# Dense passes and the first routing between the first attention and the routed tiles

## The chip, the cores and the metric

The kernel runs on one core of a Trainium2 chip. The metric is the device time of one execution in microseconds (us). The engines are named as in the profile: PE (matrix multiplies; PEld is its weight load), DVE (vector), ACT (activations), POOL (general purpose), SP (issues most DMAs).

## The reference

Two layers of gated cross attention, each followed by a mixture of experts, on 16 sequences of 112 tokens of width 256 (1792 tokens), with a context of 375 rows for each sequence:

```python
x = x + tanh(g_xattn[0]) * L0_xattn(layernorm(x), ctx)   # 16 heads of 16
x = x + tanh(g_ffn[0])   * L0_ffn(layernorm(x))
x = x + tanh(g_xattn[1]) * L1_xattn(layernorm(x), ctx)   # one head of 256
x = x + tanh(g_ffn[1])   * L1_ffn(layernorm(x))
```

The change lies in and around `L0_ffn`. It has 14 routed experts, of which each token takes two, and 2 shared ones that every token passes through. Each expert is RMS norm, 256 to 512, SiLU, 512 to 256:

```python
gates = softmax(xf @ router_w)                 # 14 logits for each token
top_v, top_i = top_k(gates, 2)                 # scattered into masked, then normalised
routed_out = einsum('end,ne->nd', routed, masked)
shared = sum over the 2 shared experts of silu(h @ W1) @ W2
```

## The kernel before

All arithmetic is float32. Tokens lie in `x_sb` in 14 tiles of 128. For the shared experts the tiles are grouped in `blocks`: (0, 4), (4, 4), (8, 4), (12, 2), that is first tile and number of tiles. One *pass* is one shared expert over one block. It consists of pieces:

- `hidden_piece` (L472): 128 of the 512 hidden columns for a block. PE multiplies into a bank (L476), ACT applies Silu into `hT` (L480). Four of them (`KH`) make a pass's hidden half.
- `output_piece` (L482): one token tile of the block. PE multiplies `hT` by the second weights (L486), DVE adds the result to `x_sb` (L490). There are as many as the block has tiles.

A float32 matmul appears as two records in the profile. A hidden piece is 4 records of L476, an output piece 8 of L486. `hT` comes from a pool with two buffers.

**First attention.** It runs as 64 steps (`last` = 64), one for each sequence and group of four heads, and some more steps that empty the pipeline. In a step `n` the order of every engine's queue is written out: scores of step `n`, work registered for place 0, `apply` of step `n - 2`, place 1, place 2, `maxima`, `turned_scores(n - 1)` (PE, then four Exp on ACT, L649), place 3. Extra work is registered with `at(step, place, ...)`. Near the end these are: `project(12)` at step 65 and `project(13)` at step 67, place 2 (L692; PE L695, DVE L699); `first_turn` of the last sequence at step 66 and `second_turn` at step 67 (L670, L682); `measured1` (statistics on DVE and powers on POOL), `normed1` (DVE, and an SP store to `xn_rows`), `turned1` (two PE transposes, an ACT copy to `xT`) and `logits` (PE, ACT into `lg0`) for each token tile; those of the last tile come at steps 67, 69, 70 and 71.

PSUM banks in a step come from `bank()` (L528). At place 2 the first three requests of a step get banks 0, 1 and 3 of the two pairs that hold the scores in full steps; a pair is one tile of two banks.

One pass, shared expert 0 over block 0, is placed in steps 65 to 72, a piece for each step (L748 to L752).

**Between attention and the routed tiles** (L907 to L952). Here nothing is pinned: a planner orders the instructions by their place in the program and by what is ready, and may also move them in between the written ones ahead. The pieces of three passes are mixed with the routing:

- `two_largest` (L239): for each token the two largest logits as one-hot rows, on DVE.
- `places` (L290): counts by matmuls (L302, L305), from them on DVE the owner of each of `TILES0` = 41 tiles of 128 rows (`owner_i`) and the row of each token (`at_i`).
- `takers` (L348): one-hot matrices on DVE (L395, L380, L386) and 56 records of small matmuls (L404) give the token in each row (`taker`).
- `gates_of` (L263): the two gate values, with one Exp on ACT (L277).

The three passes are expert 0 over block 1, expert 1 over block 0, expert 1 over block 1, with `places` behind the first pass's hidden pieces and `takers` behind the second's.

**Routed tiles** (`routed`, L851). For each tile SP loads the owner's weights (L858; it needs `owner_i`), POOL gathers 128 rows of `xn_rows` (L860; it needs `taker`), PE transposes them (L867), DVE scales (L869), then hidden (L879, L884), output (L891, L893) and a store. Tile t + 1 is fetched and transposed ahead of tile t's hidden matmuls. The weights pool has six buffers, of which the two shared experts keep two. The first 36 tiles always run, the last 5 only if needed.

After that the second layer's products, the four remaining passes over blocks 2 and 3 (`rest`), the second attention and its experts follow.

Of the kernel before, what the change touches and what calls it, by code (L numbers as in the profile page):

```python
# [19 lines left out]
NT = N // P  # L20
# [5 lines left out]
ER, ES = 14, 2  # L26
HID = 512
KH = HID // P
E1 = 4

TILES0 = 2 * NT + ER - 1
# [26 lines left out]
def tile_flamingo(  # L58
# [124 lines left out]
    tg = const.tile([P, 4], F32, tag="tg", name="tg")  # L183
# [48 lines left out]
    def at_once(parts):  # L232
        while True:
            try:
                next(parts)
            except StopIteration as end:
                return end.value

    def two_largest(wk, lg, e, nt):  # L239

        sh = [P, nt, e]

        def full(name, shape=sh):
            return wk.tile(shape, F32, tag=f"{name}{e}_{nt}", name=name, bufs=1)

        ohs, tmp, left = full("ohs", [P, nt, 2, e]), full("tmp"), full("left")
        rev = revi[:, ER - e : ER].unsqueeze(1).to_broadcast(sh)
        tops = []
        for r in range(2):
            top, first = full(f"top{r}", [P, nt]), full(f"first{r}", [P, nt])  # L250
            tops.append(top)
            nc.vector.tensor_reduce(top, lg, AX.X, ALU.max)
            nc.vector.tensor_tensor(tmp, lg, bc(top, sh), ALU.is_equal)
            nc.vector.tensor_tensor(tmp, tmp, rev, ALU.mult)
            nc.vector.tensor_reduce(first, tmp, AX.X, ALU.max)
            nc.vector.tensor_tensor(ohs[:, :, r, :], tmp, bc(first, sh), ALU.is_equal)
            if r == 0:
                nc.vector.scalar_tensor_tensor(left, ohs[:, :, 0, :], -3e38, lg, ALU.mult, ALU.add)
                lg = left
                yield  # L260
        return ohs, tops
# [28 lines left out]
    def places(wk, pool, tag, ohs, e, n, nt=NT):  # L290


        def full(name, shape, dtype=F32):
            return wk.tile(shape, dtype, tag=f"{name}{e}", name=name, bufs=1)


        both = full("both", [P, nt + 1, e])
        nc.gpsimd.memset(both[:, nt, :], 0.0)
        nc.vector.tensor_add(both[:, :nt, :], ohs[:, :, 0, :], ohs[:, :, 1, :])
        yield  # L300
        before = pool.tile([P, nt + 1, e], F32, tag=tag, name="before")
        nc.tensor.matmul(before, below, both, start=True, stop=False)  # L302
        for i in range(nt):
            sh = [P, nt - i, e]
            nc.tensor.matmul(  # L305
                before[:, i + 1 :, :], ones, both[:, i : i + 1, :].to_broadcast(sh),
                start=False, stop=(i == nt - 1),
            )
        yield

        own_i = full("own_i", [P, e], I32)
        nc.vector.tensor_scalar(own_i, before[:, nt, :], float(P - 1), None, ALU.add)
        nc.vector.tensor_scalar(own_i, own_i, 7, None, ALU.arith_shift_right)
        own = full("own", [P, e])
        nc.vector.tensor_copy(own, own_i)
        sh = [P, 2, e, e]
        up = full("up", sh)
        nc.vector.tensor_tensor(
            up, own.unsqueeze(1).unsqueeze(1).to_broadcast(sh), below_e[:, :, :e, :e], ALU.mult
        )  # L320
        ends = full("ends", [P, 2, e])
        nc.vector.tensor_reduce(ends, up, AX.X, ALU.add)

        past = full("past", [P, n, e])
        nc.vector.tensor_tensor(
            past, ends[:, 1:2, :].to_broadcast([P, n, e]), bc(marks[:, :n], [P, n, e]), ALU.is_le
        )
        owner = full("owner", [P, n])
        nc.vector.tensor_reduce(owner, past, AX.X, ALU.add)
        owner_i = keep.tile([P, n], I32, tag=f"owner_i{e}", name="owner_i")  # L330
        nc.vector.tensor_scalar(owner_i, owner, float(e - 1), None, ALU.min)
        total_i = keep.tile([P, 1], I32, tag=f"total_i{e}", name="total_i")
        nc.vector.tensor_copy(total_i, ends[:, 1, e - 1 : e])
        yield owner_i, total_i

        spot = full("spot", [P, nt, e])
        nc.vector.tensor_tensor(
            spot, before[:, :nt, :], ends[:, 0:1, :].to_broadcast([P, nt, e]), ALU.add
        )
        sh = [P, nt, 2, e]  # L340
        nc.vector.tensor_tensor(ohs, ohs, spot.unsqueeze(2).to_broadcast(sh), ALU.mult)
        at = full("at", [P, nt, 2])
        nc.vector.tensor_reduce(at, ohs, AX.X, ALU.add)
        at_i = keep.tile([P, nt, 2], I32, tag=f"at_i{e}", name="at_i")
        nc.vector.tensor_copy(at_i, at)
        return at_i
# [96 lines left out]
    blocks = [(t, min(4, NT - t)) for t in range(0, NT, 4)]  # L443
# [25 lines left out]
    def hidden_rows():  # L469
        return dense.tile([P, KH, 4 * P], F32, tag="hT", name="hT")  # L470

    def hidden_piece(new_bank, hT, e, t0, n, m):  # L472
        a = both[e][0]
        ph = new_bank()[:, : n * P]
        for k in range(KD):
            nc.tensor.matmul(  # L476
                ph, a[:, k, m * P : (m + 1) * P], xT[:, k, t0 * P : (t0 + n) * P],
                start=(k == 0), stop=(k == KD - 1),
            )
        nc.scalar.activation(hT[:, m, : n * P], ph, AF.Silu)  # L480

    def output_piece(new_bank, hT, e, t0, j):  # L482
        c, i = both[e][1], t0 + j
        py = new_bank()[:, :D]
        for m in range(KH):
            nc.tensor.matmul(  # L486
                py, hT[:, m, j * P : (j + 1) * P], c[:, m, :],
                start=(m == 0), stop=(m == KH - 1),
            )
        nc.vector.scalar_tensor_tensor(  # L490
            x_sb[:, i, :], py, tg[:, 2:3], x_sb[:, i, :], ALU.mult, ALU.add
        )

# [5 lines left out]
    with tc.tile_pool(name="a0", bufs=2) as a0, tc.tile_pool(  # L502
        name="a0_s", bufs=1, space=PSUM
# [240 lines left out]
        def at(step, where, f, *args):  # L744
            side.setdefault((step, where), []).append((f, args))


        hT = hidden_rows()  # L748
        pieces = [(hidden_piece, (bank, hT, 0, *blocks[0], m)) for m in range(KH)]
        pieces += [(output_piece, (bank, hT, 0, blocks[0][0], j)) for j in range(blocks[0][1])]  # L750
        for n, (f, args) in enumerate(pieces):
            at(last + 1 + n, 2, f, *args)  # L752

        def blank():

# [151 lines left out]
    with tc.tile_pool(name="f0", bufs=3) as f0, tc.tile_pool(  # L907
        name="f0_h", bufs=3, space=PSUM
    ) as ps_h, tc.tile_pool(name="f0_y", bufs=3, space=PSUM) as ps_y, tc.tile_pool(
        name="f0_x", bufs=2, space=PSUM  # L910
    ) as ps_x:
        ohs, tops = at_once(two_largest(f0, lg0, ER, NT))

        def h_bank():
            return ps_h.tile([P, 512], F32, tag="h", name="ph")

        def y_bank():
            return ps_y.tile([P, D], F32, tag="y", name="py")

        def run(units, after=lambda n: None):  # L920
            prev = None
            for n, (e, t0, w) in enumerate([*units, (None, None, None)]):
                if e is not None:
                    hT = hidden_rows()
                    for m in range(KH):
                        hidden_piece(h_bank, hT, e, t0, w, m)
                if prev is not None:
                    for j in range(prev[3]):
                        output_piece(y_bank, *prev[:3], j)
                if e is not None:  # L930
                    after(n)
                prev = (hT, e, t0, w)

        units = [(e, t0, w) for t0, w in blocks for e in range(ES)]
        first, rest = [units[2], units[1], units[3]], units[4:]
        found = {}

        def route(n):
            if n == 0:
                parts = places(f0, ps_x, "x", ohs, ER, TILES0)  # L940
                next(parts)
                next(parts)
                found["owner"], found["total"] = next(parts)
                found["at"] = at_once(parts)
            if n == 1:
                found["taker"] = at_once(
                    takers(f0, ps_x, "x", found["at"], ER, TILES0)
                )

        run(first, route)  # L950
        at_i, owner_i, taker, total_i = (found[name] for name in ("at", "owner", "taker", "total"))
        gates = at_once(gates_of(f0, lg0, tops, ER, NT, 1e-9, tg[:, 2:3]))  # L952

        routed(0, OFTEN0, wpool, f0, ps_h, ps_y, ps_x)

# [742 lines left out]
```

## Time and profile before

| | us |
|---|---|
| runs | 915.47, 921.25, 924.17; median 921.25 |
| profiled execution | 921.77, its span 919.8, mean granted PE clock 0.986 |
| PE busy in the span | 859.0 (93%) |
| DVE, ACT, POOL busy | 468.9, 347.0, 231.5 |
| first dense matmul after the attention's steps (L476, into `ph`) | 357.86 |
| first weight load of a routed tile issued (L858) | 373.66 |
| `taker` written (L417) | 392.72 |
| first transpose of a routed tile (L867, PE) | 414.32 |
| first hidden matmul of a routed tile (L879) | 415.32 |
| last hidden matmuls of the routed tiles | 558.9 |

Times inside the execution count from the start of the span. A row of a timeline has the start, the time from the first record's start to the last one's end, the engine, the line, the operation with output and inputs, the shape and the number of records; in brackets the idle time before it and what ended it. Busy PE is not PE at its peak, since matmuls overlap; the granted clock has to be read beside it.

ACT's rows where it changes between Exp and Silu, in the last attention steps and after them:

```profile
327.73 1.48 ACT L649 ACTIVATE pT<-pt 125x336 f32<-125x336 f32 x4 [0.87 <-PE pt L642]
330.66 0.27 ACT L738 ACTIVATE lg<-pt,rt 128x14 f32<-128x14 f32 x1 [1.46 <-PE pt L734]
330.95 1.28 ACT L480 ACT_TABLE_LOAD   x1
332.42 0.60 ACT L480 ACTIVATE hT<-sp 128x512 f32<-128x512 f32 x1 [0.18 <-PE sp L476]
...
356.39 1.28 ACT L277 ACT_TABLE_LOAD   x1 [3.74 <-DVE g L272]
357.69 0.38 ACT L277 ACTIVATE g<-g 128x210 f32<-128x210 f32 x1
359.92 1.28 ACT L480 ACT_TABLE_LOAD   x1 [1.85 <-PE ph L476]
```

Every change of function set has a load of 1.28 us in ACT's queue.

### The profile page before, as it was taken

The numbers are of one execution on the slowest core, as the hardware profiler recorded it, in microseconds if no ns is written. First come the engines' busy times: TensorE is split into PE (matmuls) and PEld (weight loads), VectorE is DVE, ScalarE is ACT, GpSimd is POOL, SyncE is SP. The second block draws the span as 40 slices with busy tenths as digits, with TensorE's granted clock in tenths as the row PEclk, the third lists the DMA queues.
The fourth block names the chain that finished last, engine by engine and source line by source line (L and its number), as shares of the span: only waits on it lengthen the run. The fifth ranks groups of instructions, "written<-read, shape, count | busy, mean of one in ns | idle before, by whom it ended". The sixth has DMA issues, their size and how long they took to land. (4 is left out here: it accounts for less than half of the span.)

```text
span 919.8 us, 18113 instructions
## 1 busy us (share of the span) xinstructions
PE 859.0 (93%) x7038; PEld 619.4 (67%) x7038; DVE 468.9 (51%) x1240; ACT 347.0 (38%) x851; POOL 231.5 (25%) x435
## 2 busy tenths in 40 slices
PE   6899999999999978999999999989999998999984
PEld 3566666666666645779888887666778776767753
DVE  3666666565566623512222223585556463666557
ACT  2455555555555432111111110223223354445453
POOL 3231221120111111013222213670433313221063
PEclk9999999999999999889999999999999999999998
DMA  7230010001010000406999995322346334899834
GB/s 262 64 94 1 25 47 25 24 24 42 25 41 9 7 9 10 183 24 225 319 318 305 320 302 159 117 69 70 121 121 188 145 138 142 287 318 334 291 82 107
DMA packets 41911, 124.02 MB, mean 135 GB/s; under 512 B 5712, under 2 KB 22224, under 8 KB 33248
## 3 DMA queue, kind: packets, MB, share of 16 engines
q1 hardware_dynamic: 35664, 108.30, 34.9%
q0 software_dynamic: 5616, 14.03, 5.6%
q8 instruction: 56, 0.92, 0.4%
q10 hardware_dynamic: 544, 0.52, 0.2%
q14 instruction: 31, 0.25, 0.1%
HBM read 109.46 MB, written 13.37 MB: 134 GB/s over the span
## 5 line engine op out<-in xcount | busy, mean ns | idle before, releaser
L621 DVE TENSOR_REDUCE mz<-sp 112x2 f32<-112x750 f32 x128 | 114.2, 935 | 56.0 <-PE sp L614 56.0
L649 ACT ACTIVATE pT<-pt 125x336 f32<-125x336 f32 x256 | 94.6, 456 | 65.0 <-PE pt L642 65.0
L207 POOL TENSOR_SCALAR rstd<-mv 128x1 f32<-128x1 f32 (+1 forms) x49 | 12.2, 250 | 300.9 <-DVE mv L200 295.2
L879 PE MATMUL phr<-xgT,wr_sb 128*128 128x128 f32 x576 | 73.2, 280 | 7.5 <-DVE xgT L869 7.5
L879 PEld LDWEIGHTS phr<-xgT,wr_sb 128*128 128x128 f32 x576 | 68.0, 191 | 12.4 <-DVE xgT L869 12.1
L1396 PE MATMUL py<-wr_sb,hT 128*128 128x256 f32 x312 | 76.1, 388 | 0.0
L860 POOL DMA_INDIRECT xg_sb<-xn_rows,taker x36 | 34.3, 954 | 155.6 <-PE px L867 108.4
L884 ACT ACTIVATE hTr<-phr 128x512 f32<-128x512 f32 x36 | 21.5, 597 | 137.1 <-PE phr L879 137.1
L869 DVE TENSOR_SCALAR xgT<-px,wr_sb 128x128 f32<-128x128 f32 x72 | 21.9, 346 | 96.5 <-DMA wr_sb<-in_wr_dram 67.3
L891 PE MATMUL pyr<-wr_sb,hTr 128*128 128x256 f32 x288 | 68.0, 379 | 0.0
L661 PEld LDWEIGHTS pt<-pT,va 125*32 125x32 f32 x1536 | 38.0, 109 | 39.1 <-ACT pT L649 33.6
L1396 PEld LDWEIGHTS py<-wr_sb,hT 128*128 128x128 f32 x312 | 57.8, 195 | 6.6
L642 PE MATMUL pt<-qm,kt 32*125 32x112 f32 x1536 | 61.2, 283 | 0.7 <-ACT kt L546 0.4
L661 PE MATMUL pt<-pT,va 125*32 125x112 f32 x1536 | 58.7, 264 | 2.0 <-ACT pT L649 2.0
L642 PEld LDWEIGHTS pt<-qm,kt 32*125 32x125 f32 x1536 | 49.1, 183 | 15.7 <-issue 11.6
L1385 ACT ACTIVATE hT<-ptz,wr_sb 128x128 f32<-128x128 f32 x156 | 57.9, 449 | 1.6 <-PE ph L1352 1.6
L614 PE MATMUL sp<-kt,qt 32*112 32x375 f32 x512 | 56.6, 494 | 1.2 <-ACT qt L573 0.8
L541 PE MATMUL pt<-ctx_sb,wk 128*128 128x375 f32 x128 | 51.6, 527 | 5.8 <-DMA ctx_sb<-in_ctxT_dram 5.8
L891 PEld LDWEIGHTS pyr<-wr_sb,hTr 128*128 128x128 f32 x288 | 52.0, 190 | 5.6
L199 DVE BATCH_NORM_STATS2 bnst<-ph 128x6 f32<-128x512 f32 x39 | 27.2, 698 | 40.0 <-PE ph L1352 39.1
L546 ACT ACTIVATE kt<-pt,bks,spots 128x375 f32<-128x375 f32 x64 | 39.0, 659 | 22.7 <-PE pt L541 22.7
L476 PE MATMUL ph<-xT,w_sb 128*128 128x512 f32 (+1 forms) x112 | 46.8, 567 | 0.6 <-DVE x_sb L490 0.6
(275 smaller groups left out, 1514.1 us busy)
## 6 DMA issues: line engine op xcount, KB each, us to landing
wr_sb<-in_wr_dram SPq DMA_DIRECT2D x36, 1025.0 KB
wr_sb<-in_wr_dram SPq DMA_DIRECT2D x31, 1028.0 KB
ctx_sb<-in_ctxT_dram SPq DMA_DIRECT2D x32, 375.0 KB
yg<-yr SPq DMA_DIRECT2D x59, 128.0 KB
ctxn_sb<-in_ctxN_dram SPq DMA_DIRECT2D x16, 375.0 KB
xn_rows<-xn SPq DMA_DIRECT2D x24, 128.0 KB
out_dram<-yb SPq DMA_DIRECT2D x10, 128.0 KB
w_sb<-in_w1s_dram SPq DMA_DIRECT2D x2, 512.0 KB
```

The source lines that it names most:

```text
L476: nc.tensor.matmul(ph, a[:, k, m * P : (m + 1) * P], xT[:, k, t0 * P : (t0 + n) * P], start=(k == 0), stop=(k == KD - 1),)
L541: nc.tensor.matmul(pk, wk0_sb[:, k, c * P : (c + 1) * P], ctxs[b][:, k, :], start=(k == 0), stop=(k == KD - 1),)
L546: nc.scalar.activation(kts[b][:, c, u, :], pk, AF.Identity, bias=bks[:, c, u : u + 1], scale=spots[:, 2 + u : 3 + u],)
L614: nc.tensor.matmul(sps[j // 2][:TQ, j % 2, :S], qt[r : r + HP, c, t0 : t0 + TQ], kt[r : r + HP, g, u, :], start=True, stop=True,)
L621: nc.vector.tensor_reduce(mz[:, 2 * h : 2 * h + 2, HD * (1 - u)], sp[:TQ, :, :S], AX.X, ALU.max, negate=True,)
L642: nc.tensor.matmul(sts[j][:SC, s * TQ : (s + 1) * TQ], kt[r : r + HP, c // 2, c % 2, s * SC : (s + 1) * SC], qm[r : r + HP, :], start=True ...
L649: nc.scalar.activation(pT[:, j, :], sts[j][:SC, : NSC * TQ], AF.Exp)
L661: nc.tensor.matmul(po[r : r + HP, :], va[:, s, (c // 2) * 8 + j * 2 + c % 2, :], pT[:, j, s * TQ : (s + 1) * TQ], start=(s == 0), stop=(s ...
L879: nc.tensor.matmul(ph[:, m, :], a[:, k, m * P : (m + 1) * P], xgT[:, k, :], start=(k == 0), stop=(k == KD - 1),)
L891: nc.tensor.matmul(py, hT[:, m, :], c[:, m, :], start=(m == 0), stop=(m == KH - 1))
L1385: nc.scalar.activation(hT[:, m, :], pt[:, m, :], AF.Relu, bias=w[:, c + KH + m : c + KH + m + 1], scale=w[:, c + m : c + m + 1],)
L1396: nc.tensor.matmul(py, hT[:, m, :], w[:, c : c + D], start=(m == 0), stop=(m == KH - 1))
```

## The change

A generator `two_passes` yields the pieces of both shared experts over a block: eight hidden ones, then all output ones. Over block 0 (16 pieces) they are placed among the attention's steps 64 to 71, two for each step, ahead of the step's other work at place 2. Over block 1 they run after the attention, now in written order: `routing` is a generator with the same steps as before, cut into parts, and behind each of the 16 pieces its next part is issued. Its first part (the first half of `two_largest`) stands before the first piece, the counting matmuls behind the third, the owners behind the fourth, the matmuls of `takers` behind pieces 10 to 13, `taker` behind the 14th, and the gates behind the 15th. The amount of arithmetic is the same: two passes over each of blocks 0 and 1, and `rest` as before.

```diff
+    def two_passes(block, h_bank, y_bank):
+
+        hTs = [hidden_rows() for _ in range(ES)]
+        for e, hT in enumerate(hTs):
+            for m in range(KH):
+                yield hidden_piece, (h_bank, hT, e, *block, m)
+        for e, hT in enumerate(hTs):
+            for j in range(block[1]):
+                yield output_piece, (y_bank, hT, e, block[0], j)
+
...
-        hT = hidden_rows()
-        pieces = [(hidden_piece, (bank, hT, 0, *blocks[0], m)) for m in range(KH)]
-        pieces += [(output_piece, (bank, hT, 0, blocks[0][0], j)) for j in range(blocks[0][1])]
-        for n, (f, args) in enumerate(pieces):
-            at(last + 1 + n, 2, f, *args)
+        for n, (f, args) in enumerate(two_passes(blocks[0], bank, bank)):
+            at(last + n // 2, 2, f, *args)
...
-        ohs, tops = at_once(two_largest(f0, lg0, ER, NT))
...
-        def run(units, after=lambda n: None):
...
-        units = [(e, t0, w) for t0, w in blocks for e in range(ES)]
-        first, rest = [units[2], units[1], units[3]], units[4:]
-        found = {}
-
-        def route(n):
-            if n == 0:
-                parts = places(f0, ps_x, "x", ohs, ER, TILES0)
-                next(parts)
-                next(parts)
-                found["owner"], found["total"] = next(parts)
-                found["at"] = at_once(parts)
-            if n == 1:
-                found["taker"] = at_once(
-                    takers(f0, ps_x, "x", found["at"], ER, TILES0)
-                )
-
-        run(first, route)
-        at_i, owner_i, taker, total_i = (found[name] for name in ("at", "owner", "taker", "total"))
-        gates = at_once(gates_of(f0, lg0, tops, ER, NT, 1e-9, tg[:, 2:3]))
+        found = []
+
+        def routing():
+            ohs, tops = yield from two_largest(f0, lg0, ER, NT)
+            parts = places(f0, ps_x, "x", ohs, ER, TILES0)
+            next(parts)
+            yield
+            yield
+            next(parts)
+            yield
+            owner_i, total_i = next(parts)
+            yield
+            at_i = at_once(parts)
+            yield
+            taker = yield from takers(f0, ps_x, "x", at_i, ER, TILES0)
+            yield
+            gates = at_once(gates_of(f0, lg0, tops, ER, NT, 1e-9, tg[:, 2:3]))
+            found.extend((at_i, owner_i, total_i, taker, gates))
+
+
+        with tc.manual_schedule():
+            parts = routing()
+            next(parts)
+            for f, args in two_passes(blocks[1], h_bank, y_bank):
+                f(*args)
+                next(parts, None)
+        at_i, owner_i, total_i, taker, gates = found
+        rest = [(e, t0, w) for t0, w in blocks[2:] for e in range(ES)]
```

More of the change, by code (lines that the diff above doesn't have):

```diff
@@ L918, in y_bank @@
             return ps_y.tile([P, D], F32, tag="y", name="py")
-        def run(units, after=lambda n: None):
[L921 to L932, printed above, removed]
```

## The prediction

> **What bounds the kernel now.** I read the slices over the span first, then the windows by stage, and then PE's timeline through the two places that the change touches. Over the span PE is 93% busy and no other engine is above 51%, so PE's order is what is worth reading. The windows show what each stage waits for (us; then busy time of PE, PEld, DVE, ACT, POOL with counts; granted clock; DMA share; GB/s):
>
> ```profile
> 334.00:342.00 8.00, 5.10 (x16) 2.05 (x16) 2.35 (x7) 1.19 (x2) 2.97 (x10) 1.00 0.00 0
> 385.00:397.00 12.00, 12.00 (x42) 8.50 (x42) 1.34 (x3) 0.60 (x1) 3.16 (x3) 0.57 0.17 59
> 440.00:470.00 30.00, 28.10 (x187) 25.24 (x187) 7.71 (x24) 4.18 (x7) 6.82 (x8) 1.00 0.95 321
> ```
>
> In the attention's last steps (first row) PE works 64% of the time: this is the gap that the change fills. Between attention and the routed tiles (second row) PE is always busy but its clock is at 0.57. In the routed tiles (third row) the DMA engines are 95% busy with expert weights; that stage runs at the pace of its loads, each of which waits for an earlier tile's buffer. So when the routed stage starts decides when it ends, and a shift of its start is carried to the end of the kernel. The whole question is where the first routed tile starts: 414.3 us now.
>
> PE's timeline of the attention's last steps, with the stall before each group in brackets:
>
> ```profile
> 330.42 1.96 PE L476 MATMUL sp<-xT,w_sb 128*128 128x512 f32 x4
> 333.06 1.13 PE L695 MATMUL sp<-wo,oT 128*128 128x256 f32 x4 [0.69 <-ACT hT L480]
> 334.84 1.98 PE L476 MATMUL sp<-xT,w_sb 128*128 128x512 f32 x4 [0.65 <-DVE x_sb L699]
> 337.51 0.65 PE L674 MATMUL sp<-ident,oS 128*112 128x128 f32 x4 [0.69 <-ACT hT L480]
> ...
> 352.51 1.99 PE L486 MATMUL sp<-w_sb,hT 128*128 128x256 f32 x8 [0.23 <-DVE x_sb L490]
> 355.23 1.99 PE L486 MATMUL sp<-w_sb,hT 128*128 128x256 f32 x8 [0.72 <-DVE x_sb L490]
> 357.86 4.56 PE L476 MATMUL ph<-xT,w_sb 128*128 128x512 f32 x10 [0.64 <-DVE x_sb L490]
> ```
>
> A hidden piece is the x4 of L476, an output piece the x8 of L486. The projection (L695) and the turn (L674) write the other half of the pair of banks that the hidden piece used, and still wait for its Silu: the pair is waited for as a whole. So the cadence of dependent pieces here is 333.06 - 330.42 = 2.64 us for hidden and 355.23 - 352.51 = 2.72 us for output ones.
>
> The same view between attention and routed tiles:
>
> ```profile
> 379.81 2.75 PE L486 MATMUL py<-w_sb,hT 128*128 128x256 f32 x12
> 382.40 3.66 PE L404 MATMUL pn<-number,here 128*128 128x41 f32 x32
> 385.89 1.82 PE L476 MATMUL ph<-xT,w_sb 128*128 128x512 f32 x2
> 387.50 5.18 PE L404 MATMUL pn<-number,here 128*128 128x41 f32 x24
> 392.48 4.76 PE L476 MATMUL ph<-xT,w_sb 128*128 128x512 f32 x6
> ```
>
> 32 records of L404 take 3.5 us (to 385.89); the next 24 take 5.0 and the hidden records double, from 0.43 to 0.85 us apart. That is the halved clock.
>
> **The change, part by part.**
>
> *One more pass among the attention's last steps.* Steps 64 to 71 now take two pieces each, where steps 65 to 72 took one. I lay PE's queue out anew from the old 326.38 (after the transposes of step 64), with the cadences above. Step 64: two hidden pieces, 2.64 + 1.96, ahead of turned_scores(63): these 4.6 us delay it. Its Exp now follows a Silu, so ACT loads a table (1.28 us in the rows of this trace) between them, and apply(63), which came 0.84 us after the first Exp, runs at about 333.9 instead of 328.57 (+5.3). Step 65: two pieces (the Silu table comes back during the first, hidden), the projection in the free bank: 340.1 instead of 333.06 (+7.0). Step 66: two pieces, one of whose stalls the projection hides; the first turn at 345.5 (+8.0). Step 67: the second projection at 351.65 instead of 341.87 (+9.8). Steps 68 to 71: eight output pieces 2.7 apart, with turns and logits between and one DVE wait of 1.0 before the last turn, as now: the last piece starts at 373.5, its eviction lets the next pools start at 376.15 instead of 357.86. So the tail grows by **+18.3** for a pass. Queues: ACT and DVE get the pass's four Silus and four evictions, whose latency is in the cadences; POOL's normalising chain (3.4 us) finishes well before its normed1 two steps later; SP's last xn_rows stores go out 14 to 16 us later, long ahead of the gathers that read them.
>
> *One pass less in front of the routed tiles.* There hidden pieces run 1.745 us apart (357.86 to 364.83 for four) and output pieces 1.725 (400.51 to 414.3 for eight): 4 x 1.745 + 4 x 1.725 = **-13.9**.
>
> *The halved clock.* The stretch now is 414.3 - 357.86 = 56.4 us. At full speed it holds 12 x 1.745 + 12 x 1.725 + 3.7 (the counting matmuls, 364.83 to 368.52) + 56 x 0.109 = 6.1 (L404) = 51.4. So 5.0 us are lost to the clock. The Trainium skill ("TensorE: Matmul & The Clock Gate", Part 1 and "HAM oscillation") has the clock halve after an idle window of about 3.4 us and full again after a busy one. Taken literally it speaks against any saving here: PE's row shows no idle gap near that, so the loss would have another cause and stay, and the sum would be +6.5. The trace shows the clock at 1.00 until 386 and at 0.50 after, right behind 3.5 us of matmuls with only 41 columns, so such a stretch counts as nearly idle. In the change these matmuls come in groups of 16 records (1.8 us) with a piece of full matmuls between; the counting matmuls, 3.7 us of up to 196 columns, left the clock at 1.00. I take the trace: **-5.0**; bounds 0 and -5.0.
>
> *Written order of the routing.* The first two_largest steps now run behind the last eviction at 376.1 (they began at 352.69 among the last pieces). DVE needs about 2.1 + 2.3 us until the pair counts are there (380.5); PE reaches the counting matmuls after three pieces, at 381.3: hidden, with 0.8 to spare. Owners: 385.0 + 3.5 = 388.7 instead of 372.9. SP's four weight loads start then, took some 12 us, and are there by 402, needed at 415: hidden. The one-hot steps (1.3, 1.3, then 1.15 each) lie between evictions of 0.48; by my layout each match is ready 1 to 3 us before PE sums it. PE ends its sixteenth piece at 376.15 + 27.8 + 3.7 + 6.1 = 413.8. DVE writes the takers behind the fourteenth piece, at 411.1 (392.7 now, with 21 us of cover, which is gone). The first gather issues at 411.6; in this trace the first ran from 393.23 and its data stopped moving at about 396.0, 2.8 us; the second issues 1.55 later. PE transposes two tiles before the first routed hidden matmul, so that waits for both: 411.6 + 1.55 + 2.8 + 0.3 = 416.2, against 415.32 now. And the gates (L271 to L287: 0.4 of DVE, a table load 1.28 and Exp 0.38 on ACT, 1.6 of DVE) stand behind piece 15 in DVE's queue with the last eviction after them, to about 416.9; if the first xgT stands behind those, the first hidden is at 417.5. So the hand-over is late by 0.9 to 2.2 after the sums above; I take 1.5 as the whole.
>
> *Sum* as a check: +18.3 - 13.9 - 5.0 = -0.6 on PE's own queue, plus the wait for the gathers that takes its place, 2.1: **+1.5 us**. *Tables:* two more loads in the tail and one swap around the gates. The trace has 356.39 to 357.69 from the load's start to the Exp, 1.30; the skill ("ScalarE: Activation LUTs", What ACT_TABLE_LOAD costs) states 1.28 plus about 1.38 of drain for each switch, which the rows don't show. With it the one exposed switch at step 64 and the one at the gates would make the sum about +4. I keep the row.
>
> Against the profiled execution (921.77, span 919.8): 923.3. It stands 0.5 above the median of 921.25; I say **923**.
>
> **The rivals.**
>
> *The pair's halves are not really in conflict.* Then some ten waits in the tail vanish, 0.9 each (2.64 - 1.745): -9, together 914. For it: two hidden pieces use different banks. Against it: four different lines (L695, L674, L476, L486) show the same 0.65 to 0.72 behind the other half's reader. 0.12.
>
> *The clock still falls once in the routing block*, by groups of thin matmuls and waits around them: no saving, +6.5, 928. 0.14.
>
> *Slower: the hand-over drops the clock.* Between piece 16 (413.8) and the first routed hidden matmul (416.2 to 417.5) PE has nothing but four transposes. If that is counted as an idle window, the routed stage begins at half clock; the drop in this trace lasted 10.4 us and cost 5.0. Alone 928; where the wait is also longer than I have it, by a gather or DVE order late by 5 more, 933. It decides over 1% only from about 8 us beyond my sum, that is with a PE gap of 5 us or more there. 0.14.
>
> **How the numbers follow.** My case 0.60, 919 to 927 by its own uncertainty (tail 2 us, hand-over 2, runs 2). A change of 1%, 9.2 us, is what a measurement of this kernel tells from no change. Below 912: a part of the first rival, 0.08. Above 930.5: the last rival in its dearer form, 0.12 of its 0.14, and 0.04 from the upper ends of the second and of my own case: 0.16. Within: 0.76. The range reaches to both rivals' centres at the lower side and the 1% line above: 915 to 931.
>
> **What would show it.** Right: the first dense matmul after attention 17 to 20 us later than 357.86; pieces 2.6 to 2.7 apart from step 64 on; clock 1.00 through the routing; px behind the gathers with a PE gap of 1 to 4 us; routed stage of the same 150 us. Wrong: pieces 1.8 apart in the tail, a clock of 0.5 anywhere from 376 to 425, or px placed ahead of the last pieces so that PE waits for gathers with work behind it.

## The result, and the profile after

The changed kernel takes 926.62 us in the median of 13 runs (922.78 to 929.54), against 921.86 of the kernel before (13 runs, 913.78 to 928.16). The ratio is 1.0054, with a 95% interval from 1.0030 to 1.0078: slower by 5 us, clearly more than nothing and less than 1%. Ratios here and below leave out single executions that took over 1.5% longer than the fastest of their kernel. The profiled execution took 926.03 us, its span is 924.3.

PE's timeline of the changed kernel in the attention's last steps (L652 is `turned_scores`, L671 `apply`, L744 the logits, L705 the projection, L684 the first turn; these are the old lines 642, 661, 734, 695 and 674):

```profile
326.65 1.88 PE L476 MATMUL sp<-xT,w_sb 128*128 128x512 f32 x4
329.22 1.98 PE L476 MATMUL sp<-xT,w_sb 128*128 128x512 f32 x4 [0.69 <-ACT hT L480]
331.14 0.92 PE L652 MATMUL pt<-qm,kt 32*125 32x112 f32 x24
334.26 1.51 PE L671 MATMUL pt<-pT,va 125*32 125x112 f32 x24 [2.20 <-ACT pT L659]
335.70 1.03 PE L744 MATMUL pt<-router,xT 128*128 128x14 f32 x4
336.57 3.76 PE L476 MATMUL sp<-xT,w_sb 128*128 128x512 f32 x4
341.02 3.78 PE L476 MATMUL sp<-xT,w_sb 128*128 128x512 f32 x4 [0.69 <-ACT hT L480]
344.59 1.61 PE L705 MATMUL sp<-wo,oT 128*128 128x256 f32 x4
346.04 1.88 PE L476 MATMUL sp<-xT,w_sb 128*128 128x512 f32 x4
...
377.54 1.99 PE L486 MATMUL sp<-w_sb,hT 128*128 128x256 f32 x8 [0.97 <-DVE x_sb L490]
380.18 5.42 PE L476 MATMUL ph<-xT,w_sb 128*128 128x512 f32 x12 [0.64 <-DVE x_sb L490]
```

`apply` waits 2.20 us for the Exp, and the two hidden pieces behind it take 3.76 and 3.78 us where the others take 1.88 to 1.98. ACT's rows show why PE waited: the Exp stands behind two Silu and a table load.

```profile
328.57 0.60 ACT L480 ACTIVATE hT<-sp 128x512 f32<-128x512 f32 x1
331.24 0.60 ACT L480 ACTIVATE hT<-sp 128x512 f32<-128x512 f32 x1 [2.07 <-PE sp L476]
332.12 1.28 ACT L659 ACT_TABLE_LOAD   x1 [0.28 <-PE pt L652]
333.41 1.48 ACT L659 ACTIVATE pT<-pt 125x336 f32<-125x336 f32 x4
```

The windows show what that wait did to PE (us; busy time of PE, PEld, DVE, ACT, POOL; granted clock; DMA share; GB/s):

```profile
332.00:334.00 2.00, 0.06 (x4) 0.00 (x0) 0.00 (x0) 1.87 (x3) 0.00 (x0) 1.00 0.00 0
334.00:336.00 2.00, 1.74 (x26) 1.11 (x26) 0.20 (x1) 0.90 (x3) 0.00 (x0) 0.88 0.00 0
336.00:338.00 2.00, 2.00 (x6) 1.39 (x6) 0.08 (x1) 1.15 (x2) 0.00 (x0) 0.50 0.00 0
...
344.00:346.00 2.00, 2.00 (x5) 1.26 (x5) 0.00 (x0) 0.60 (x1) 0.00 (x0) 0.56 0.00 0
346.00:348.00 2.00, 1.92 (x5) 0.58 (x4) 1.09 (x3) 0.04 (x1) 0.42 (x2) 1.00 0.00 0
```

Behind the idle stretch the clock is halved from about 335.5 to 345.8, for 10.24 us: a window of 2 us with a mean of 0.88 holds 0.48 us at half speed, one with 0.56 holds 1.76, and there are 8 us between them. The routing block, in contrast, keeps its clock. PE's timeline there, down to the first routed tile (L874 is the transpose of gathered rows, L886 the routed hidden matmul; old lines 867 and 879):

```profile
401.41 1.98 PE L404 MATMUL pn<-number,here 128*128 128x41 f32 x16
403.21 1.97 PE L486 MATMUL py<-w_sb,hT 128*128 128x256 f32 x8
405.02 1.88 PE L404 MATMUL pn<-number,here 128*128 128x41 f32 x16
...
412.86 5.43 PE L486 MATMUL py<-w_sb,hT 128*128 128x256 f32 x24
418.95 0.41 PE L874 MATMUL px<-ident,xg_sb 128*128 128x128 f32 x2 [0.66 <-DMA xg_sb<-xn_rows,taker]
420.50 0.41 PE L874 MATMUL px<-ident,xg_sb 128*128 128x128 f32 x2 [1.14 <-DMA xg_sb<-xn_rows,taker]
420.75 3.51 PE L886 MATMUL phr<-xgT,wr_sb 128*128 128x128 f32 x16
```

Here 16 records of L404 take 1.9 us each time, full speed. Then PE waits for both gathers, and in this execution the clock falls once more: 3.51 us for the first 16 routed records, where later tiles have 1.95.

To compare traces I count from the transposes of step 64 (L728, now L738), since executions reach them up to 3 us apart:

| trace | transposes to first dense matmul | from there to first routed hidden | sum |
|---|---|---|---|
| before | 326.01 to 357.86: 31.9 | to 415.32: 57.5 | 89.3 |
| before, second trace (e9) | 31.9 | 57.5 | 89.3 |
| after | 326.38 to 380.18: 53.8 | to 420.75: 40.6 | 94.4 |
| after, second trace (e10) | 53.9 | 40.7 | 94.6 |

The tail (from the transposes to the first dense matmul) grew by 21.9 to 22.0 us, the block behind it shrank by 16.8 to 16.9, and the difference, 5.1 to 5.2, is close to the 4.8 between the medians. What follows varies between executions of one kernel: from the first routed hidden matmul to the first of the second layer's products 148.4 and 150.3 us in the two traces of before, 152.1 and 147.4 in those of after; so a single span is not to be read to a few us, and ratios over many runs are given below.

### The profile page after: what moved, and what is told of

It reads as the page before. It is cut to its first block, busy times and chain, and to the rows that moved or that the text cites. A ratio compares the mean times of both kernels' runs of the same rounds, so it can differ in the third digit from the quotient of the medians.

```text
span 924.3 us, 18108 instructions
## 1 busy us (share of the span) xinstructions
PE 857.1 (93%) x7038; PEld 616.2 (67%) x7038; DVE 469.9 (51%) x1240; ACT 350.8 (38%) x853; POOL 232.2 (25%) x435
## 5 line engine op out<-in xcount | busy, mean ns | idle before, releaser
L886 PE MATMUL phr<-xgT,wr_sb 128*128 128x128 f32 x576 | 74.2, 283 | 10.2 <-DVE xgT L876 10.1
L886 PEld LDWEIGHTS phr<-xgT,wr_sb 128*128 128x128 f32 x576 | 69.2, 195 | 14.3 <-DVE xgT L876 14.1
L671 PEld LDWEIGHTS pt<-pT,va 125*32 125x32 f32 x1536 | 38.0, 109 | 40.6 <-ACT pT L659 35.1
L671 PE MATMUL pt<-pT,va 125*32 125x112 f32 x1536 | 58.8, 264 | 3.4 <-ACT pT L659 3.4
L652 PE MATMUL pt<-qm,kt 32*125 32x112 f32 x1536 | 60.7, 283 | 0.7 <-ACT kt L556 0.4
L652 PEld LDWEIGHTS pt<-qm,kt 32*125 32x125 f32 x1536 | 48.7, 183 | 16.1 <-issue 12.2
L551 PEld LDWEIGHTS pt<-ctx_sb,wk 128*128 128x128 f32 x128 | 22.7, 198 | 32.2 <-ACT pT L659 16.6
```

The costliest lines, as they stand in the source:

```text
L551: nc.tensor.matmul(pk, wk0_sb[:, k, c * P : (c + 1) * P], ctxs[b][:, k, :], start=(k == 0), stop=(k == KD - 1),)
L652: nc.tensor.matmul(sts[j][:SC, s * TQ : (s + 1) * TQ], kt[r : r + HP, c // 2, c % 2, s * SC : (s + 1) * SC], qm[r : r + HP, :], start=True ...
L671: nc.tensor.matmul(po[r : r + HP, :], va[:, s, (c // 2) * 8 + j * 2 + c % 2, :], pT[:, j, s * TQ : (s + 1) * TQ], start=(s == 0), stop=(s ...
L886: nc.tensor.matmul(ph[:, m, :], a[:, k, m * P : (m + 1) * P], xgT[:, k, :], start=(k == 0), stop=(k == KD - 1),)
```

## The experiments

In all of them the reference is the kernel before, run on the same chip; ratios are to it. The changed kernel has 1.0054.

**e1, e8: the passes one step later.**

```diff
-            at(last + n // 2, 2, f, *args)
+            at(last + 1 + n // 2, 2, f, *args)
```

> The changed kernel with the two passes over block 0 one step later (steps 65 to 72), so that no Silu stands before the Exp of step 64. Theory (the Exp waited for two pieces and a table load, PE stood for 2.2 us before apply, and the clock was then halved for some 10 us): one table load less on each side of the Exp, wait before apply(63) back to 0.8 us, granted clock 1.00 through the tail, first dense matmul after the attention near 374.5 in place of 380.2, total about 921 (5 to 6 below the changed kernel). Rival (the clock falls because pieces 2.6 us apart leave PE too idle on the whole, wherever they begin): the clock still falls to 0.5 in the tail and the first dense matmul stays near 379 to 381, total 925 to 927.

> The kernel of e1_later once more, since its timed runs were few and wide apart while its trace showed the tail 4.5 us shorter with the clock at 1.00. Theory: ratio to before 1.000 to 1.003 (2 to 5 below the changed kernel's 1.0054). Rival (the time won in the tail is lost later): ratio 1.005 or more again.

Measured: 1.0102 (1.0059 to 1.0145, only six runs) and then 1.0034 (1.0005 to 1.0064). In e1's trace `apply` waits 0.75 us and no piece is slow: from the transposes to the first dense matmul 49.3 us in place of 53.8. In e8's trace two pieces are slow all the same, and the sum is 55.1:

```profile
327.61 2.02 PE L671 MATMUL pt<-pT,va 125*32 125x112 f32 x24 [0.55 <-ACT pT L659]
329.56 1.03 PE L744 MATMUL pt<-router,xT 128*128 128x14 f32 x4
330.43 3.76 PE L476 MATMUL sp<-xT,w_sb 128*128 128x512 f32 x4
```

There the clock is at 0.50 already from 322.7 on, ahead of everything that the change touches, and stays there for 17 us; why it fell in this execution and not in e1's is not shown. So e1's trace agrees with the theory (no wait of 2.2 us, no fall), and e8's shows that removing this wait does not exclude a fall. In the total no gain is shown: the two measurements of this one kernel lie 6 us apart, one above the changed kernel's 1.0054 and one below it, and the 6 us that I expected did not come.

**e2: dense work in the wait.** Pieces 3 and 4 go ahead of `apply` in step 65, the projection to a free bank:

```diff
-                return score_bank((0, 1, 3)[n])
+                return score_bank(place["banks"][n])
...
-            at(last + n // 2, 2, f, *args)
+            if n in (2, 3):
+                args = (lambda j=n - 2: score_bank(j), *args[1:])
+            at(last + n // 2, 0 if n in (2, 3) else 2, f, *args)
...
-            place["pair"] = {}
+            place.update(pair={}, banks=(3, 1, 0) if n == last + 1 else (0, 1, 3))
```

> The changed kernel with pieces 3 and 4 of block 0 issued ahead of apply(63) in step 65, so that PE has dense work while ACT loads the Exp table and computes the four Exp. The table loads stay as they are. Theory (the gap in PE halves the clock, not the table loads): wait before apply(63) under 0.5 us, clock 1.00 in the tail, first dense matmul after the attention 374 to 376, total 920 to 923. Rival (the table switches themselves cost the time): as late as now, 379 to 381, total 925 to 927.

Measured: 1.0034 (1.0010 to 1.0057), and a trace that does not tell the two apart, because the wait only moved:

```profile
331.02 1.99 PE L476 MATMUL sp<-xT,w_sb 128*128 128x512 f32 x4
335.89 2.82 PE L476 MATMUL sp<-xT,w_sb 128*128 128x512 f32 x4 [2.88 <-ACT hT L480]
338.64 1.35 PE L671 MATMUL pt<-pT,va 125*32 125x112 f32 x24
```

Piece 3's Silu now stands behind the table load, the four Exp and a second load, and piece 4 waits for it in the shared pair of banks. The clock falls behind that wait too, for a shorter time (0.66 over 336 to 341, that is 3.4 us at half speed). That agrees with the idle time as the cause, but I had missed the second table load in laying the edit out. In this execution the clock had fallen once before, for 3.4 us from 323.3 on, as in e8 ahead of what the change touches.

**e3: the second bank from the other pair.**

```diff
-                return score_bank((0, 1, 3)[n])
+                return score_bank(place["banks"][n])
...
-            place["pair"] = {}
+            place.update(pair={}, banks=(0, 3, 1) if n >= last else (0, 1, 3))
```

> The changed kernel with the second request for a bank at place 2 of a step from 64 on taken from the other pair (banks 0, 3, 1 in place of 0, 1, 3). Theory (a pair of banks is waited for as a whole, 0.6 to 0.7 us for each piece): the waits before L476 and L486 in the tail fall from some ten to at most three, pieces come 1.7 to 2.0 us apart, first dense matmul after the attention 6 to 8 us earlier than 380.2 (the halved clock at step 65 stays), total 918 to 921. Rival (the waits are for the last reader's latency, whichever bank it is): no wait goes, total 925 to 928.

Measured: 0.9972 (0.9948 to 0.9997), some 7.6 us under the changed kernel. The pieces run together in pairs, as PE's timeline of e3 shows:

```profile
333.14 1.45 PE L671 MATMUL pt<-pT,va 125*32 125x112 f32 x24 [2.20 <-ACT pT L659]
334.52 0.62 PE L744 MATMUL pt<-router,xT 128*128 128x14 f32 x4
334.99 5.38 PE L476 MATMUL sp<-xT,w_sb 128*128 128x512 f32 x8
...
347.20 3.61 PE L476 MATMUL sp<-xT,w_sb 128*128 128x512 f32 x8
...
352.92 3.62 PE L486 MATMUL sp<-w_sb,hT 128*128 128x256 f32 x16
```

Eight records of L476, two pieces, in 3.6 us without a wait between, where one piece with its wait took 2.6. The tail is 43.7 us (53.8). So the pair is waited for as a whole, and that makes a pass dear there. Not all of the 10 us are these waits. The halved clock behind `apply` is in this trace too, but it lasts 3.4 us (0.6 in the first window, 2.8 in the second) and not 10.24, which is worth up to 3.4 us:

```profile
331.00:336.00 5.00, 2.86 (x30) 1.88 (x31) 0.28 (x1) 3.51 (x7) 0.00 (x0) 0.94 0.00 0
336.00:341.00 5.00, 5.00 (x11) 2.14 (x9) 0.00 (x0) 2.00 (x3) 0.00 (x0) 0.72 0.00 0
341.00:346.00 5.00, 4.26 (x14) 1.92 (x12) 1.09 (x3) 0.92 (x2) 2.84 (x9) 1.00 0.00 0
```

The clean pair is e1 and e7 (below), both with the clock at 1.00 through the tail: 49.3 and 40.9 us. There the other bank is worth 8.4 us.

**e4: the takers one piece earlier.**

```diff
-                next(parts, None)
+                for _ in range(2 if n == 7 else 1):
+                    next(parts, None)
```

> The changed kernel with two parts of the routing behind piece 8, so that every later part comes one piece earlier (matmuls of takers behind pieces 9 to 12, the takers behind piece 13, the gates behind 14). Theory (PE stands at the hand-over for the two gathers, and the clock then falls): first gather issued some 3.5 us earlier against the end of the last piece, first routed hidden matmul at most 0.7 us behind the last output piece in place of 2.5, clock 1.00 there in place of 0.5 from 420.7 to 424, total 3 to 4 below the changed kernel, 922 to 924. Rival (the routed stage is bound by its weight loads, so a start 3 us earlier is lost again): start earlier by 3, total within 1 of 926.6.

Measured: 1.0064 (1.0043 to 1.0086). The trace has what was expected of the hand-over: first gather ready with the last piece, 38.6 us from first dense to first routed hidden in place of 40.6. But half of these two us is lost at once, because after two records PE waits for scaled rows, whose scaling stands behind two evictions in DVE's queue:

```profile
418.25 0.46 PE L886 MATMUL phr<-xgT,wr_sb 128*128 128x128 f32 x2
419.42 1.83 PE L886 MATMUL phr<-xgT,wr_sb 128*128 128x128 f32 x14 [0.71 <-DVE xgT L876]
```

From the first dense matmul to the end of the first 16 routed records it is 41.6 us, against 42.6 in e10, the trace of the changed kernel without a fall at this place. One us is within what the intervals leave open; I expected 3 to 4, and no gain is shown.

**e5: the tail alone.** The two passes in steps 64 to 71 as in the change, the block behind them left to the planner as before, with two passes (of the edit against the kernel before, the line for the block):

```diff
-        first, rest = [units[2], units[1], units[3]], units[4:]
+        first, rest = [units[2], units[3]], units[4:]
```

> Half of the change alone: both passes over block 0 in steps 64 to 71, and behind the attention the two passes over block 1 with the routing left to the planner, as in the kernel before. Theory (the tail costs 22 for a pass that costs 13.9 elsewhere, 4 of it by the halved clock; the written order is what removes the second halving): clock 0.5 near step 65 and again behind the takers' matmuls, total 6 to 9 above before, ratio 1.007 to 1.010, that is slower than the whole change. Rival (the planner's order was as good as the written one): ratio 1.003 to 1.006, as the whole change.

Measured: 1.0051 (1.0018 to 1.0085). The tail alone is as slow as the whole change, and not slower, as I had expected. In its trace the planner's order of the block is the better one by 1.9 us (38.7 from first dense to first routed hidden, against 40.6): it keeps 28 output records behind the last of L404, which cover the gathers, and the clock did not fall:

```profile
404.31 3.66 PE L404 MATMUL pn<-number,here 128*128 128x41 f32 x32
407.80 1.11 PE L486 MATMUL py<-w_sb,hT 128*128 128x256 f32 x4
408.75 2.77 PE L404 MATMUL pn<-number,here 128*128 128x41 f32 x24
411.34 6.29 PE L486 MATMUL py<-w_sb,hT 128*128 128x256 f32 x28
```

**e6: the written order alone.** One pass in steps 65 to 72 as before; behind it the 24 pieces of three passes in written order, a part of the routing behind each of the first ones:

```diff
+        def three_passes():
...
+            for part in (hidden(0), hidden(1), output(0), hidden(2), output(1), output(2)):
+                yield from part
...
-            for f, args in two_passes(blocks[1], h_bank, y_bank):
+            for f, args in three_passes():
```

> The other half alone: one pass in steps 65 to 72 as before, and behind the attention three passes (24 pieces) in written order with a part of the routing behind each of the first pieces, the takers behind the 14th, ten pieces left to cover the gathers. Theory (the halved clock behind the takers' matmuls costs 5.0 and the written order removes it; the gathers are hidden): clock 1.00 from the attention's end to the routed tiles, first routed hidden matmul about 52 us behind the first dense one in place of 57.5, total 3 to 5 below before, ratio 0.995 to 0.997. Rival (the clock's fall there is chance and the written order's waits take its place): ratio 0.999 to 1.002.

Measured: 0.9955 (0.9930 to 0.9981). Clock at 1.00, 52.7 us from first dense to first routed hidden in place of 57.5, and ten pieces behind the takers cover the gathers. Written order with three passes, which is not quite the change's block of two, is a gain of 4 us.

**e7: later and other pair together** (the edits of e1 and e3).

> The changed kernel with both edits in the tail: the two passes one step later, and the second bank of a step from the other pair. Theory (the Exp behind a Silu and the pair that is waited for as a whole are separate costs of about 4 and 7): clock 1.00 in the tail, waits before the pieces gone, first routed hidden matmul 11 to 13 us earlier than in the changed kernel (counted from the transposes of step 64), ratio to before 0.990 to 0.995. Rival (a start of the routed tiles earlier than before is lost again in that stage, which is paced by its loads): ratio 0.997 to 1.000 although the routed tiles start 7 us earlier than before.

Measured: 0.9964 (0.9940 to 0.9987). The tail is 40.9 us with the clock at 1.00; transposes to first routed hidden 81.6, 12.8 below the changed kernel. By the trace that is 7.7 below before, by the runs only 3.3 (1.2 to 5.5). In this trace nothing of the earlier start is lost later, against the rival: from the first routed hidden matmul to the end of the span it is 504.5 us, and 504.5 and 502.9 in the two traces of before. But the execution is not typical: it is the second fastest of 22 (911.63, median 916.18), and its mean granted clock is 0.992 where that of the 22 is 0.985. Where the others lose the rest stays open.

**e9, e10: both kernels once more, for a second trace.**

> The kernel before once more, for a second trace. Theory (the matmuls of takers, 3.5 us with 41 columns, halve the clock whenever they run in one stretch): clock 0.5 for some 10 us behind them again, L404's last 24 records near 5 us in place of 2.8. Rival (whether the clock falls depends on how the stretch lies against a window that runs by itself): the fall is absent or elsewhere in this trace.

> The changed kernel once more, for a second trace. Theory: PE stands 2.2 us before apply(63) again (this is set by the order of ACT's queue), the clock falls behind it again, hidden pieces 3 and 4 take some 3.8 us each. Rival: the wait is there but the clock stays at 1.00, and the first dense matmul comes 4 us earlier, counted from the transposes of step 64.

Both halved clocks come again at the same places. Behind `apply` in e10:

```profile
334.00:336.00 2.00, 2.00 (x23) 1.52 (x22) 0.28 (x1) 0.09 (x1) 0.00 (x0) 0.52 0.00 0
336.00:338.00 2.00, 2.00 (x5) 1.09 (x5) 0.00 (x0) 1.45 (x2) 0.00 (x0) 0.50 0.00 0
```

And behind L404 in e9, the second trace of before:

```profile
382.57 3.66 PE L404 MATMUL pn<-number,here 128*128 128x41 f32 x32
386.06 1.62 PE L476 MATMUL ph<-xT,w_sb 128*128 128x512 f32 x2
387.48 5.18 PE L404 MATMUL pn<-number,here 128*128 128x41 f32 x24
```

The fall at the hand-over comes and goes. In e10 the first 16 routed records take 1.95 us behind the same wait for gathers, and so they do in e1, e2, e7 and e8; in e3 they take 3.57 us, as in the first trace of the change (3.51).

**e11, e12: versions that beat both kernels.** e11 is e6 with e3's banks; e12 is the changed kernel with e1's, e3's and e4's edits.

> The kernel of e6_written_only (one pass in the tail, three passes in written order behind it) with the second bank of a step from the other pair. Theory: three to five waits of 0.65 to 0.7 us in the tail go, the rest is as in e6, ratio to before 0.991 to 0.995. Rival (the tail of one pass is set by the chain from the last projection to the last logits, so these waits are covered): ratio as e6, 0.995 to 0.997.

> The changed kernel with all three edits: two passes one step later, the second bank from the other pair, takers one piece earlier. Theory (the wait for the gathers, 2.5 us in e7's trace, is a cost of its own): first routed hidden matmul 1.5 to 2.5 us nearer to the last output piece than in e7, ratio to before 0.992 to 0.995. Rival (e4's result holds: nothing is won by earlier takers): ratio 0.996 to 0.997 as e7.

Measured: e11 0.9908 (0.9873 to 0.9943), e12 0.9872 (0.9815 to 0.9929, six runs, one of them left out). In e11 the tail is 28.3 us (e6: 32.1), so the chain from the last projection to the last logits did not cover all of the waits. In e12 the sum is 79.4 us with the clock at 1.00 up to the routed tiles. That is 2.2 us less than in e7, while the ratio is lower by some 8 us; so few runs don't show how much of that is the earlier takers, and e4 alone showed no gain from them. The intervals of e11 and e12 overlap; which of the two is faster stays open, that both beat the kernel before does not.

## Why the prediction came out as it did

I said 923, 1.5 above the profiled execution of before, with a range from 915 to 931 and most of the chance within 1%. The measured 926.6 lies in it, and the direction is right; the size is 5 in place of 1.5. Two signs went against me: the first dense matmul came 22.3 us later and not 17 to 20, and the clock of 0.5 that I had named as a sign of being wrong between 376 and 425 stood in the profiled execution from 420.9 on.

**The pass in the tail** was put at +18.3 and is +22.0. This is the term that was mis-sized. My layout had the wait itself: `apply` at 333.9 (it came at 334.26), the table load between Silu and Exp, the first dense matmul at 376.15 (it came at 380.18). What it had not was the consequence: pieces 3 and 4 at 3.76 and 3.78 us in place of about 1.9, 3.7 in sum, with a slower projection behind them. I had named an idle PE as what halves the clock, and looked for it only at the hand-over. That the fall belongs to this wait: it stands right behind it in all five traces that have the wait in this form (after, e3, e4, e5, e10), and in none of before, e1, e6, e7, e9, e11 and e12; e8's began earlier. That the fall explains the 3.7 us is read from traces; the runs of e1 and e8, where the wait is gone, do not show the gain in the total. The reason for the cadence, the shared pair, was right, and e3 shows it; the cadence itself was a little shorter than the 2.6 to 2.7 us that I took (329.22 - 326.65 = 2.57 for hidden pieces, 2.47 to 2.97 for output ones). The rival that the halves are not in conflict falls.

**The pass removed, the clock in the routing block and the gathers**: -13.9 - 5.0 and +2.1 for the hand-over make -16.8; the two traces have -16.9 and -16.8. Owners, weight loads and the one-hot chain were hidden as laid out, the gates too: the first scaling of a routed tile went ahead of the last of them in DVE's queue. The rival in which the clock still falls in the block falls: no trace in written order shows it.

But the -5.0 were booked to the written order, and e5 says that this isn't the whole of it: with one pass less the planner's order did not lose them either, in the one trace there is, and covered the gathers. So in this change the written order gained nothing over the planner's that the runs show; with three passes (e6), which leave ten pieces behind the takers in place of two, it gains 4 us over before. Tail and written order measured alone, 1.0051 and 0.9955, therefore don't add up to the change's 1.0054.

**The slower rival**, a clock that falls at the hand-over, happened in the profiled execution (some 1.6 us) and in e3's trace, and not in e10. It was the right mechanism at the less important place.

**The start of the routed tiles carried to the end**: within a trace it holds. From the first routed hidden matmul to the end of the span all traces but e3's take 500 to 508 us, however early they come there; why e3's takes 514 is open. Between traces and runs it holds well for the change, e2, e6 and e11, less well for the others, and for e1 not at all (us; the first column is the sum of the first table less the 89.3 of before, the second comes from the ratios):

| | start of the routed tiles, one trace | total, runs | rest of the span, same trace |
|---|---|---|---|
| before, e9 | 0 | 0 | 504.5, 502.9 |
| after, e10 | +5.1, +5.2 | +5.0 | 503.6, 504.5 |
| e1 | +0.5 | +9.4 | 507.7 |
| e8 (the same kernel) | +6.6 | +3.1 | 500.2 |
| e2 | +2.6 | +3.1 | 505.9 |
| e3 | -5.1 | -2.6 | 513.7 |
| e4 | +3.0 | +5.9 | 505.3 |
| e5 | +2.9 | +4.7 | 507.0 |
| e6 | -4.5 | -4.1 | 504.3 |
| e7 | -7.7 | -3.3 | 504.5 |
| e11 | -8.3 | -8.5 | 507.4 |
| e12 | -9.9 | -11.8 | 507.9 |

## What to carry to other kernels

When work is laid into the gaps of a latency-bound stretch, cost it at that stretch's cadence, and look for what its results do to the other queues: a Silu ahead of an Exp cost two table loads, and the wait behind it cost more by the clock than by itself. Before filling gaps, look at why the pieces wait on one another; here a different choice of bank, an edit of two lines, was worth 7.6 us where the whole change cost 5. And measure the halves of a change alone: here one gained 4 us and the other lost 5, and they did not add up.

## What the hardware showed

- In all 14 traces the granted clock on record was either full or half, and every stretch at half speed that ended before the span did lasted a whole multiple of 3.41 us: 3.41 (e2, e3), 6.83, 10.24 (before, after, e4, e5, e9, e10) or 17.07 (e8). The falls within one trace are whole multiples apart, too: those of the changed kernel, at 335.5 and 420.9, 25 of them. So the clock changed only at points 3.41 us apart, which lay differently against the program in every execution: behind the start of `apply` the fall came after 0.6 us in e10 and 2.2 us in e3.
- A gap of 2.2 us in PE, between thin matmuls, was enough to halve the clock, in five traces of five. In the trace of the change the 3.41 us ahead of the fall hold 2.15 us of idle PE and 1.26 us of `apply`. The half speed lasted 10.24 us in four of the five, where the next pieces stood 0.69 us apart, and 3.41 us in e3, where they ran without a gap. The Trainium skill ("TensorE: Matmul & The Clock Gate", Part 1) has a window of about 3.4 us for the fall as for the recovery; the multiples above agree with it, and a fall here needed much less than a whole window of idle PE.
- 3.5 us of matmuls with 41 columns, without an idle gap of more than 0.5 us, did the same in both traces of before. In e5 the same 32 records did not. The kind and number of the records behind the 32 (two of L476, in e5 four of L486) are hardly the reason: in the traces of before the fall came at 386.15 and 386.52, when only 0.3 and 0.5 us of them had run. It may be how the stretch lay against the points, which fell 3.75 and 3.95 us behind its start in the two traces of before and 2.8 us behind it in e5 (worked out from the fall at 335.4 there). The same would explain why equal waits at the hand-over halved the clock in two traces of seven. No run tests it, and where the limit lies I can't say.
- In e2 and e8 the clock fell in the last full attention steps, with PE's waits no longer than 0.75 us. Falls at such and later places are a part of the several us by which executions of one kernel differ: the six fastest of e7's 22 (911.4 to 913.0 us) have mean clocks of 0.985 to 0.993, the six slowest (918.0 to 921.2) of 0.980 to 0.983.
